# A graph layer and attention in float32: block products of the projections replaced by float32r products

## The chip, the cores and the metric

The kernel runs on one core of a Trainium2 chip. The metric is device time in microseconds from launch to end, as the median of several runs. The engines are TensorE (PE, with its weight loads shown as PEld), VectorE (DVE), ScalarE (ACT), GpSimd (POOL) and SyncE (SP), which issues most DMAs.

## What is computed

Input are 64 batches of 256 nodes with 512 features, and one graph of 256 nodes. Two layers follow, each with a residual and a layer norm. Cut to what matters:

```
# layer 0
mi, mj = x @ Wi.T, x @ Wj.T
out = deg * (mi + b) + adj @ mj
x = layernorm(x + out)
# layer 1, 8 heads of 64
q, k, v = (split_heads(x @ W.T + b) for W, b in ((Wq, bq), (Wk, bk), (Wv, bv)))
scores = where(adj == 0, -inf, q @ k.T / 8)
out = (softmax(scores) @ v) @ Wo.T + bo
x = layernorm(x + out)
```

Everything is float32. The products with Wq, Wk, Wv and Wo are the projections q, k, v and o.

## The kernel before

Two batches form a group, and there are 32 groups. All loops are unrolled; the order of the instructions on TensorE is written out by hand, since `matmul` (L290) keeps each in program order. `in_order` does the same for an instruction of another engine; other instructions, passed through `anywhere` or not wrapped at all, are placed by the framework's scheduler.

**Layer 0** (`l0_steps`). Each batch makes mi and mj by block products in Strassen's manner: seven products (steps 1 to 7) in place of eight, over sums `xS` of blocks of the transposed x (`sum_x`) and combined weights `w0`. Steps 1 and 3 share a PSUM bank x, steps 4 and 6 a bank y, steps 5 and 7 a bank z, and step 2 has a bank w. There are three slots for such banks (`bank`), two double banks for scores (`score_banks`) and one for attention values (`value_bank`). mj is split into two float32r parts, hi and lo (`split`), which `neighbours` multiplies with the graph, also float32r. `take` and `give` add and normalise the result, and `send_h` sends it through DRAM so that it comes back in columns, which `turn_h` transposes on DVE into `hT`.

**Projections** (`pair_steps`, `qkv_steps`, `qk_steps`, `v_steps`, `o_steps`). A group's two batches are the two block rows of a matrix of 512 rows; each projection has seven block products again, over sums `hS` (for q, k, v) or `oS` (for o). The right factors are blocks of a weight or differences of blocks; `make_factors` makes the differences once and keeps them in DRAM. `bring` loads factors of 256 KB from DRAM in the order of `queue`, eight ahead, and each is used by one step. The results are put together from the banks and from kept partial products (tag u) by DVE, ACT and POOL.

**Attention** (`scores`, `values`, `divide_two`, `multiply`). For each pair of heads, w from 0 to 7 in a group: scores on TensorE, mask on DVE (L809), exponential on ACT (L813), sum of two key halves on POOL (L816); then the values, the denominators `den`, a reciprocal on DVE (L886), eight small DMAs that spread it over the partitions, and a product on POOL (L848).

**The main loop** runs over the groups: the attention of group g is mixed with layer 0 of group g+1, and after it stand o of group g and q, k, v of group g+1, mixed with the end of layer 0 of the group's second batch b2. The first group has a prologue, the last an end of its own.

Of the kernel before, what the change touches and what calls it, by code (L numbers as in the profile page):

```python
# [224 lines left out]
def unshifted_path(ctx, tc, flag, x, adj, wiT, wjT, b0, wqT, bq, wkT, bk, wvT, bv, woT, bo, out):  # L225
# [27 lines left out]
    AHEAD = 8  # L253
# [6 lines left out]
    p4 = ctx.enter_context(tc.tile_pool(name="p4", bufs=4))  # L260
    p6 = ctx.enter_context(tc.tile_pool(name="p6", bufs=6))
    stream = ctx.enter_context(tc.tile_pool(name="stream", bufs=AHEAD + 1))
# [35 lines left out]
    def load_x(b):  # L298
        if b < B:
            xh[b] = p6.tile([P, NT, D], F32, tag="xh", name="xh")  # L300
            nc.sync.dma_start(out=xh[b], in_=x[b].rearrange("(t p) d -> p t d", p=P))

    b_bc = p4.tile([P, D], F32, tag="u", name="b_bc")
# [20 lines left out]
    xT, xS, hT, hS, qT, kT, vv, aoT, oS = ({} for _ in range(9))  # L324


    ident = const.tile([P, P], F32, name="ident")
# [15 lines left out]
    aT = p3.tile([P, NT, N], F32, tag="pk", name="aT")  # L343
    deg = small.tile([P, NT], F32, tag="deg", name="deg")
# [16 lines left out]
    def check_graph():  # L361


        exact = p1.tile([P, NT, N], F32, tag="oS", name="exact")
        in_order(nc.vector.tensor_tensor(exact, aT, graph.bitcast(F32), ALU.not_equal))
        in_order(nc.vector.tensor_reduce(inexact, exact.rearrange("p t n -> p (t n)"), AX.X, ALU.max))
        in_order(nc.vector.tensor_scalar(maskT, aT, 0.0, MASK, ALU.is_equal, ALU.mult))
# [9 lines left out]
    def load_bias(b, name):  # L377
        t = const.tile([P, NC], F32, tag=name, name=name)
        nc.sync.dma_start(out=t, in_=b)
        d = const.tile([P, 2], F32, tag=name + "d", name=name + "d")  # L380
        return t, d

    bq_sb, bqd = load_bias(bq, "bq")
    bk_sb, bkd = load_bias(bk, "bk")

    def bias_steps():
        for t, d in ((bq_sb, bqd), (bk_sb, bkd)):
            in_order(nc.vector.tensor_sub(d, t[:, 2:4], t[:, 0:2]))

    bv_t = small.tile([P, NC], F32, tag="bvt", name="bv_t")  # L390
# [5 lines left out]
    def blocks_of(w):  # L396
        return (w.rearrange("(h c p) (j o) -> p h c j o", h=2, p=P, j=2) if w is woT else
                w.rearrange("(p h c) (j o) -> p h c j o", h=2, p=P, j=2))

    sources = {}  # L400
    for name, w in (("wq", wqT), ("wk", wkT), ("wv", wvT), ("wo", woT)):
        src = blocks_of(w)
        sources[name] = {B11: src[:, 0, :, 0], B21: src[:, 1, :, 0], B22: src[:, 1, :, 1]}


    def load_raw(w, tag):
        raw = p1.tile([P, 2, 2, 2, H], F32, tag=tag, name="raw")
        nc.sync.dma_start(out=raw.rearrange("p h c j o -> p (h c) (j o)"),
                          in_=w.rearrange("(c p) o -> p c o" if w is woT else "(p c) o -> p c o", p=P))
        return raw  # L410

    def make_factors(w, name, raw):
        kept = dram.tile([4, P, 2, H], F32, tag=name, name=name)
        t1, t2, t3, t4 = (p4.tile([P, 2, H], F32, tag="u", name="t") for _ in range(4))
        b11, b12, b21, b22 = (raw[:, h, :, j, :] for h in range(2) for j in range(2))
        for n, (t, p, m) in enumerate(((t1, b12, b11), (t2, b22, t1), (t3, b22, b12), (t4, b21, t2))):
            in_order(nc.vector.tensor_sub(t, p, m))
            nc.sync.dma_start(out=kept[n], in_=t)
        sources[name].update({T1: kept[0], T2: kept[1], T3: kept[2], T4: kept[3]})

    spread = p3.tile([P, NC, P], F32, tag="pk", name="spread")
# [3 lines left out]

    def fold_value_bias(raw):

        pb = score_bank("pb")
        for c in range(NC):
            h, kc = divmod(c, 2)  # L430
            matmul(pb, spread[:, c], raw[:, h, kc].rearrange("p j o -> p (j o)"),
                   start=(c == 0), stop=(c == NC - 1))
        nc.vector.tensor_add(bo_bc, pb, bo_bc)
# [4 lines left out]
    def bring():  # L438
        if queue:
            name, n = queue.pop(0)  # L440
            f = stream.tile([P, 2, H], F32, tag="factor", name="factor")
            nc.sync.dma_start(out=f, in_=sources[name][n])
            coming.append(f)

    def next_factor():
        f = coming.pop(0)
        bring()
        return f


    def norm_stats(t, order=anywhere):
# [3 lines left out]
        nc.vector.bn_aggr(mv, st)  # L455
        ve = small.tile([P, 1], F32, tag="ve", name="ve")
        nc.vector.tensor_scalar(ve, mv[:, 1:2], EPS, None, ALU.add)
# [3 lines left out]
        nc.gpsimd.tensor_tensor(rstd, ve, mhalf, ALU.pow)  # L461
# [40 lines left out]
    def l0_steps(b, late=False):  # L502
        banks, k = {}, {}
        order = in_order if late else anywhere
# [19 lines left out]
        def split(t):  # L524
            nc.scalar.copy(k["hi"][:, t, :], k["mj"][:, t, :])
            nc.gpsimd.tensor_tensor(k["lo"][:, t, :], k["mj"][:, t, :], k["hi"][:, t, :].bitcast(F32),
                                    ALU.subtract)

        def step1():
            product("x", raw(0, 0), B11, True)  # L530
            nc.scalar.copy(keeper("u1"), banks["x"])

        def step2():
            product("w", raw(1, 1), T4, True)
            add_scaled(1, banks["w"])

        def step3():
            product("x", raw(0, 1), B21, False)
            add_scaled(0, banks["x"])

        def step4():
            product("y", xS[b]["S2"], T2, True)
            nc.vector.tensor_add(keeper("u2"), banks["y"], k["u1"])

        def step5():
            product("z", xS[b]["S1"], T1, True)
            k["mj"] = p1.tile([P, NT, D], F32, tag="mj", name="mj")
            nc.vector.tensor_copy(k["mj"][:, 1, :], banks["z"])

        def step6():  # L550
            product("y", xS[b]["S3"], T3, False)
            nc.vector.tensor_add(keeper("u3"), banks["y"], k["u1"])
            nc.gpsimd.tensor_tensor(k["mj"][:, 1, :], k["mj"][:, 1, :], k["u3"], ALU.add)

# [3 lines left out]
            if not late:  # L558
                add_scaled(1, k["u3"])

        def step7():
            product("z", xS[b]["S4"], B22, False)
            order(nc.vector.tensor_add(k["mj"][:, 0, :], banks["z"], k["u2"]))
# [11 lines left out]
        def take(t):  # L575
            r = xh[b][:, t, :]
            if late and t == 1:
                in_order(add_scaled(1, k["u3"]))
            in_order(nc.vector.tensor_add(r, k["pa"][:, t, :], r))
            stats[t] = norm_stats(r, in_order)  # L580

        def give(t):
# [3 lines left out]
        return [step1, step2, step3, step4, step5, step6, step7, neighbours, lambda: take(1), lambda: take(0),  # L586
                lambda: give(1), lambda: send_h(b, 1), lambda: give(0), lambda: send_h(b, 0)]

    def new_h(g):
        hT[g] = p1.tile([P, NC, NB * N], F32, tag="hT", name="hT")  # L590
        hS[g] = pair_blocks(hT[g], "hS")

    def sum_h(g):
        for step in left_steps(hS[g], in_order):
            step()
# [3 lines left out]
    def send_h(b, t):  # L599
        i = b % NB  # L600
        if t == 1:
            h_cols[b] = dram.tile([D // P, N, P], F32, tag=f"h{i}", name="h_cols")
        nc.sync.dma_start(out=h_cols[b][:, t * P:(t + 1) * P, :].rearrange("q p n -> p q n"),
                          in_=xh[b][:, t, :].rearrange("p (q n) -> p q n", n=P))
        if t == 0:
            hB[b] = p1.tile([P, N // R, P], F32, tag="hB", name="hB")
            nc.sync.dma_start(out=hB[b].rearrange("p a n -> p (a n)"),
                              in_=h_cols[b].rearrange("q (r a) n -> (q r) (a n)", r=R))

    def turn_h(b):  # L610
        g, i = divmod(b, NB)
        if i == 0:
            new_h(g)
        transposed(hT[g][:, :, i * N:(i + 1) * N], hB.pop(b))
        if i == NB - 1:
            sum_h(g)

    def h_transpose(b, t, borrow=False):
# [4 lines left out]
        pt = (score_banks("pt_h")[:, 0, :] if borrow else bank("pt_h")).rearrange("p (c n) -> p c n", c=NC)  # L623
        for c in range(NC):
            transpose(pt[:, c, :], xh[b][:, t, :].rearrange("p (n c) -> p c n", c=NC)[:, c, :], ident)
        nc.scalar.copy(hT[g][:, :, i * N + t * P:i * N + (t + 1) * P], pt)  # L626
        if t == 0 and i == NB - 1:
            sum_h(g)
# [6 lines left out]
    def pair_blocks(m, tag):  # L635

        s = p1.tile([P, 4, 2, N], F32, tag=tag, name=tag)
        return left_blocks(m[:, 0:2, 0:N], m[:, 2:4, 0:N], m[:, 0:2, N:2 * N], m[:, 2:4, N:2 * N], s)

    def block_product(bank, left, right, flip, first):  # L640


        for m in range(2):
            ms = slice(m * P, (m + 1) * P)
            for kc in range(2):
                lhsT, rhs = (right[:, kc, ms], left[:, kc, :]) if flip else (left[:, kc, ms], right[:, kc, :])
                matmul(bank[:, m, :], lhsT, rhs, start=(first and m == 0 and kc == 0),
                                 stop=(m == 1 and kc == 1), skip_group_check=True)

    def pair_steps(left, flip, use, early=False):  # L650


        banks, keepers = {}, {}

        def new_keeper(name):
            pool, tag = (p3, "lu") if early and name == "u1" else (p4, "u")
# [461 lines left out]
```

## Time and profile before

| What | Value |
|---|---|
| median of 3 runs | 3070.72 us (3069.8 to 3071.19) |
| profiled execution | 3068.79 us |
| its span, first to last instruction | 3066.9 us |
| mean granted TensorE clock | 0.999 |
| DMA | 447.54 MB, 146 GB/s over the span |
| one turn of the main loop, from 1460.92 us | 94.4 us |

"Busy" is the time in which an engine runs at least one instruction; matmuls overlap in the pipeline, so the distance from the start of one to the start of the next is what one costs. In a group of instructions, the number after the bar is the busy time, then the mean length of one in ns, then the idle time of the engine just before, with what ended it.

### The profile page before, as it was taken

How to read it: one execution, taken by the hardware profiler on the slowest of the kernel's cores; microseconds unless marked ns; L12 is line 12 of the kernel's file. 1: busy time of each engine (PE TensorE's matmuls, PEld its weight loads, DVE VectorE, ACT ScalarE, POOL GpSimd, SP SyncE). 2: the span in 40 equal slices, each digit the busy share in tenths (PEclk: the TensorE clock that was granted, in tenths of full speed). 3: DMA queues.
4: the chain of work that ended last, by engine and by line, in shares of the span. 5: the costliest groups of instructions: out<-in, count | busy, mean ns of one | idle time of the engine just before them, and what ended most of it. 6: DMA issues, size and time to landing. Idle time of an engine off the chain costs nothing. (4 is left out here: it accounts for less than half of the span.)

```text
span 3066.9 us, 46810 instructions
## 1 busy us (share of the span) xinstructions
PE 3036.6 (99%) x16646; PEld 2124.6 (69%) x16646; DVE 2178.3 (71%) x3298; ACT 974.1 (32%) x1861; POOL 1519.5 (50%) x1255
## 2 busy tenths in 40 slices
PE   7999999999999999999999999999999999999998
PEld 4667766677766777666776667776677766677665
DVE  6776677766777667777677777677766777767775
ACT  2323333323333333332233332333333333323332
POOL 2544545544545445464454554454544546445453
PEclk9999999999999999999999999999999999999999
DMA  7455544455444555345553445544455444555333
GB/s 255 123 151 159 169 121 136 132 161 166 144 125 127 159 170 155 116 133 154 161 168 119 126 145 160 167 134 134 127 158 170 151 121 128 159 161 166 120 111 96
DMA packets 410411, 447.54 MB, mean 146 GB/s; under 512 B 40896, under 2 KB 300224, under 8 KB 409792
## 3 DMA queue, kind: packets, MB, share of 16 engines
q1 hardware_dynamic: 410176, 444.50, 48.8%
q8 instruction: 136, 2.23, 0.3%
q14 instruction: 99, 0.81, 0.1%
HBM read 340.79 MB, written 70.25 MB: 134 GB/s over the span
## 5 line engine op out<-in xcount | busy, mean ns | idle before, releaser
L461 POOL TENSOR_TENSOR rstd<-ve,mhalf 128x1 f32<-128x1 f32 x256 | 140.5, 552 | 707.3 <-DVE below L459 707.3
L816 POOL TENSOR_TENSOR pk<-pe 128x512 f32<-128x512 f32 x256 | 323.1, 1278 | 322.2 <-ACT pe L813 322.2
L290 PE MATMUL po<-w,xS 128*128 128x512 f32 x1024 | 462.2, 599 | 0.7 <-DVE xS L478 0.7
L290 PE MATMUL st<-hS,factor 128*128 128x256 f32 x2048 | 453.2, 379 | 1.5 <-DVE u L689 1.2
L290 PEld LDWEIGHTS st<-hS,factor 128*128 128x128 f32 x2048 | 388.4, 190 | 56.3 <-DVE xh L744 1.7
L813 ACT ACTIVATE pe<-pe 128x1024 f32<-128x1024 f32 x256 | 270.8, 1058 | 364.4 <-DVE pe L809 364.4
L290 PE MATMUL po<-w,xT 128*128 128x512 f32 x768 | 352.1, 601 | 14.8 <-DVE xS L477 9.3
L290 PE MATMUL st<-hT,factor 128*128 128x256 f32 x1536 | 352.5, 379 | 0.7 <-ACT hT L626 0.7
L290 PEld LDWEIGHTS po<-w,xS 128*128 128x128 f32 x1024 | 189.6, 190 | 235.6 <-issue 206.3
L809 DVE TENSOR_TENSOR pe<-ps,maskT 128x1024 f32<-128x1024 f32 x256 | 298.0, 1195 | 35.4 <-PE ps L290 35.4
L290 PEld LDWEIGHTS st<-hT,factor 128*128 128x128 f32 x1536 | 291.9, 190 | 41.8 <-ACT hT L626 0.9
L886 DVE RECIPROCAL rden<-den 128x256 f32<-128x256 f32 x127 | 222.5, 1752 | 76.6 <-PE den L290 73.6
L290 PEld LDWEIGHTS po<-w,xT 128*128 128x128 f32 x768 | 144.2, 191 | 181.9 <-issue 162.8
L887 POOL TENSOR_TENSOR rtot<-rtot,rden 128x256 f32<-128x256 f32 x127 | 106.8, 841 | 320.1 <-DVE rden L886 320.1
L290 PE MATMUL ps<-qT,kT 64*128 64x256 f32 x2048 | 265.0, 393 | 0.0
L290 PE MATMUL pav<-pe,v_sb 128*32 128x256 f32 x4096 | 248.4, 382 | 1.9 <-ACT pe L813 1.9
L290 PEld LDWEIGHTS ps<-qT,kT 64*128 64x128 f32 x2048 | 184.5, 186 | 78.1 <-issue 38.6
L744 DVE TENSOR_TENSOR xh<-st,xh 128x512 f32<-128x512 f32 x186 | 144.5, 777 | 132.2 <-PE st L290 132.2
L290 PE MATMUL st<-factor,hS 128*128 128x256 f32 x1024 | 234.8, 382 | 0.0
L290 PEld LDWEIGHTS pav<-pe,v_sb 128*32 128x32 f32 x4096 | 119.8, 110 | 164.3 <-issue 95.4
L290 PE MATMUL st<-factor,oS 128*128 128x256 f32 x992 | 224.2, 379 | 0.0
L290 PEld LDWEIGHTS st<-factor,hS 128*128 128x128 f32 x1024 | 192.1, 190 | 35.2 <-issue 10.6
(115 smaller groups left out, 4648.2 us busy)
## 6 DMA issues: line engine op xcount, KB each, us to landing
xB<-in_x_dram SPq DMA_DIRECT2D x256, 128.0 KB, 3.9
xh<-in_x_dram SPq DMA_DIRECT2D x64, 512.0 KB, 4.2
factor<-wq SPq DMA_DIRECT2D x128, 256.0 KB, 4.2
factor<-wk SPq DMA_DIRECT2D x128, 256.0 KB, 2.8
factor<-wv SPq DMA_DIRECT2D x128, 256.0 KB, 2.6
spread<-rden SPq DMA_DIRECT2D x1016, 32.0 KB, 1.9
factor<-wo SPq DMA_DIRECT2D x124, 256.0 KB, 3.2
h_cols<-xh SPq DMA_DIRECT2D x124, 256.0 KB, 3.0
```

Of the source, the lines that this page charges most:

```text
L290: in_order(nc.tensor.matmul(*args, **kw))
L461: nc.gpsimd.tensor_tensor(rstd, ve, mhalf, ALU.pow)
L744: nc.vector.tensor_add(dst, src, dst)
L809: nc.vector.tensor_add(pe.rearrange("p j t q -> p j (t q)"), ps.rearrange("p j t q -> p j (t q)"), maskT.rearrange("p t q -> p (t q)").uns ...
L813: in_order(nc.scalar.activation(flat, flat, AF.Exp, scale=QSCALE, accum_out=etot[:, NB * g + i, pr:pr + 1]))
L816: nc.gpsimd.tensor_tensor(pk, pe[:, :, 0, :], pe[:, :, 1, :], ALU.add)
L886: nc.vector.reciprocal(rden, den)
L887: nc.gpsimd.tensor_tensor(rtot, rtot, rden, ALU.add)
```

## The change

**Projections in three float32r products.** Each operand A is split into a head, A x (1 - 2^-13) rounded to float32r; a low part, A - head; and a diff, head x (1 + 2^-12) - A. A weight tile f holds, likewise, its head, its low part times 2^12 (lift), and lift - head. Two sums are made: X = head·f_head + low·f_lift and Y = diff·f_diff, and the result is X x (1 + 2^-12) + Y. Each of the three products is one float32r matmul of 512 columns; the block products, the sums hS and oS, the kept partial products and `make_factors` go. A weight tile is [128, 3, 512], 768 KB, and a ring of six such tiles is loaded ahead. In the first group `make` builds each tile on ACT and DVE from the raw weight, and stores it in DRAM; later groups load it.

**Who splits.** The head is made on ACT, diff on DVE, low on DVE or POOL. h now comes back from DRAM as two halves (two loads), and each half is transposed, then split.

**Layer 0** runs its products in the order 1, 2, 3, 4, 6, 5, 7, so that mj's first half is made by one DVE add from bank z and u3 (before: a copy and a POOL add). One of the two lo parts of a batch goes from POOL to DVE.

**Order.** Nearly all vector operations, and the DMA issues of factors and of h, are pinned to program order. Four of the eight spread DMAs of a group's last division are issued by ACT. The first products of the following group's first batch are brought forward into the present group's end, and the last product of k stands after the first two scores. The value bias is folded in the first turn of the main loop, no longer in the prologue. Buffers change: p1, p3 and p5 take over from p4 and p6, rden and spread have one buffer, pk two.

The core of the diff:

```diff
-            nc.vector.tensor_copy(k["mj"][:, 1, :], banks["z"])
+            in_order(nc.vector.tensor_add(k["mj"][:, 1, :], banks["z"], k["u3"]))
...
+    def split_head(parts, src):
+        in_order(nc.scalar.activation(parts[0], src, AF.Identity, scale=DOWN))
+
+    def split_diff(parts, src):
+        in_order(nc.vector.scalar_tensor_tensor(parts[2], parts[0].bitcast(F32), UP, src, ALU.mult, ALU.subtract))
+
+    def split_low(parts, src, engine):
+        in_order(engine.tensor_tensor(parts[1], src, parts[0].bitcast(F32), ALU.subtract))
...
+    def make(f, name, j):
+        head, lift, diff = (f[:, i, :].rearrange("p (c o) -> p c o", c=NC) for i in range(3))
+        low = p3.tile([P, NC, P], F32, tag="lu", name="low")
+        for cs, raw in pieces(name, j):
+            in_order(nc.scalar.activation(head[:, cs], raw, AF.Identity, scale=DOWN))
+            in_order(nc.vector.tensor_sub(low[:, cs], raw, head[:, cs].bitcast(F32)))
+            in_order(nc.scalar.activation(lift[:, cs], low[:, cs], AF.Identity, scale=LIFT))
+        in_order(nc.vector.scalar_tensor_tensor(diff, low, LIFT, head.bitcast(F32), ALU.mult, ALU.subtract))
+        nc.sync.dma_start(out=kept[name][j], in_=f.bitcast(F32))
...
+    def pair(kind):
+        if kind == "S":
+            both = score_banks("pxy")
+            return both[:, 0, :], both[:, 1, :]
+        return bank("px"), value_bank("py") if kind == "A" else bank("py")
+
+    def rows_of_product(banks, parts, t, f, c):
+        X, Y = banks
+        head, low, diff = (d[:, c, t * P:(t + 1) * P] for d in parts)
+        first, end = c == 0, c == NC - 1
+        matmul(X, head, f[:, 0, :], start=first, stop=False, skip_group_check=True)
+        matmul(Y, diff, f[:, 2, :], start=first, stop=end, skip_group_check=True)
+        matmul(X, low, f[:, 1, :], start=False, stop=end, skip_group_check=True)
...
+    def v_step(g, i, t, kind, last):
...
+            in_order(nc.scalar.activation(dst, X, AF.Identity, scale=UP))
+            in_order(nc.vector.tensor_add(dst, Y, dst))
...
+    def o_steps(g, kinds, between):
...
+            in_order(nc.vector.scalar_tensor_tensor(r, X, UP, r, ALU.mult, ALU.add))
+            in_order(nc.vector.tensor_add(r, Y, r))
...
+        o = o_steps(g, "SMAS", [lambda: split_three(*turn_h(b2, 1), nc.vector),
+                                lambda: split_three(*turn_h(b2, 0), nc.vector)])
+        o[0]()
+        split_three(*turn_h(b1, 1), nc.gpsimd)
+        o[1]()
+        split_three(*turn_h(b1, 0), nc.gpsimd)
+        run([o[2], v[0]])
+        sum_x(b3)
+        v[1]()
+        turn_x(b3 + 1)
+        run([v[3], v[2], end[0], q_[0], end[1], k[0], end[2], q_[1], end[3], k[1], end[4]])
```

## The prediction

> **What bounds the kernel now.** I read the page's busy times first, then the costliest groups, then TensorE's timeline over one loop turn, then the windows of that turn. Busy times and the groups of the projections (busy us, mean ns of one, idle before):
>
> ```profile
> PE 3036.6 (99%) x16646; PEld 2124.6 (69%) x16646; DVE 2178.3 (71%) x3298; ACT 974.1 (32%) x1861; POOL 1519.5 (50%) x1255
> ...
> L290 PE MATMUL st<-hS,factor 128*128 128x256 f32 x2048 | 453.2, 379 | 1.5 <-DVE u L689 1.2
> ...
> L290 PE MATMUL st<-hT,factor 128*128 128x256 f32 x1536 | 352.5, 379 | 0.7 <-ACT hT L626 0.7
> ```
>
> TensorE is never short of work: the groups hardly idle. But "busy" counts overlapping pipelines, so what one matmul costs is read from start to start, in the timeline (start us, length, instruction):
>
> ```profile
> 1462.57 0.58 PE L290 MATMUL pa<-hi,graph 128*128 128x512 f32 x1
> 1462.99 0.39 PE L290 MATMUL pa<-lo,graph 128*128 128x512 f32 x1
> ...
> 1464.39 0.40 PE L290 MATMUL pa<-lo,graph 128*128 128x512 f32 x1
> 1464.62 1.89 PE L290 MATMUL st<-hT,factor 128*128 128x256 f32 x8
> 1466.35 1.89 PE L290 MATMUL st<-factor,aoT 128*128 128x256 f32 x8
> 1468.07 5.34 PE L290 MATMUL st<-hT,factor 128*128 128x256 f32 x24
> 1473.25 1.89 PE L290 MATMUL st<-factor,aoT 128*128 128x256 f32 x8
> ```
>
> One plain float32 matmul is two instructions (layer 0 has 4 products x 2 chunks x 64 batches = 512 on xS, and the page counts 1024), and 8 instructions take 1.73 us, so 0.216 us for one with 256 columns. The float32r matmuls of `neighbours` (hi and lo against graph, 512 columns) are one instruction each: 7 from 1462.99 to 1464.62, 0.234 us each. That is the price on which the change rests. The windows show the turn: projections with b2's neighbours, then attention, then both (busy us of PE, PEld, DVE, ACT, POOL; clock; DMA share; GB/s):
>
> ```profile
> 1460.92:1513.37 52.45, 52.45 (x253) 45.57 (x250) 36.24 (x64) 16.08 (x33) 23.11 (x20) 1.00 0.71 207
> 1513.37:1555.29 41.92, 41.92 (x273) 20.82 (x271) 31.09 (x39) 14.22 (x26) 24.37 (x21) 1.00 0.24 69
> 1460.92:1555.29 94.37, 94.37 (x524) 66.39 (x520) 67.33 (x103) 30.31 (x59) 47.48 (x40) 1.00 0.50 146
> ```
>
> A turn takes 94.4 us and TensorE fills it; DVE, next, is at 71%. So the time is the sum of TensorE's start-to-start intervals, and a cut there counts as long as no other engine opens a hole.
>
> [...]
>
> **The change part by part.** Times are against the profiled execution: 3068.8 us, of which 3066.9 is the span; the median of the runs is 1.9 above it.
>
> **Projection matmuls.** Before: 2048+1536+1024+992+768+744 = 7112 instructions x 0.216 = 1536.2 us. After: a group of two batches needs 48 each for q, k and v (4 outputs x 4 chunks x 3 products) and 48 for o. 32 groups x 144 + 31 x 48 = 6096 x 0.234 = 1426.5 us. **Gain 109.7 us**; per turn 48.4 less 44.9, 3.5 us. The spacing of 234 is from the same form (512 moving columns, fresh weights each time), so I keep it[...]. The LDWEIGHTS (188 ns) still fits under it.
>
> **DVE, per group.** Off: eight sums hS and oS, six u adds, three more (L696), L700, each 0.69; L720 4 x 0.48; L744 5 x 0.69 + 1.22: 19.0 us. On: Y adds of q, k, v 12 x 0.69; o 4 x 0.75 + 4 x 0.69; `split_diff` of h 4 x 0.8 (bounds: 0.69 as a plain add, 1.03 as the slowest L521 from SBUF) and of ao 1.4 + 2 x 0.8; lows 4 x 0.69: 23 us. Net +4, so 67.3 to about 71.5 of a 92 us turn, 78%. Hidden by TensorE on average.
>
> **ACT, per group.** Off: L715 12 x 0.47, L733 and L747 4 x 0.59: 8.0. On: 8 x 0.7, 4 x 0.58, heads 4 x 0.58, 1.0, 2 x 0.58, four DMA issues of some 0.6 (SP's eight take 4.95 us): 14.8. From 30 to 37 of 92: hidden. Queued behind the four issues are `give2` and a head; o's second half needs that head some 3 us later than I find it ready, so this is nothing unless that slack goes.
>
> **POOL, per group.** Off: L697 3 x 1.27, L553 2 x 1.5, L750 and L751 3.6, one lo a batch 2 x 1.38: 13.2. On: lows 4 x 1.28 + 2.4: 7.5. From 47 to 42: hidden.
>
> **Layer 0 in the order 4, 6, 5, 7.** A copy (L548) becomes an add of the same 0.69; L553 leaves the way to hi. ACT waited 240 us in all for it, but TensorE waited only 0.2 us for lo, so: nothing.
>
> **DMA.** Before, 28 factors of 256 KB a turn; after, 16 of 768 KB: 7.3 to 12.6 MB, in all some 160 MB more, 447 to 610 MB, about 203 GB/s over the span against the 351 to 424 GB/s of the busiest early windows. The ring of six is short at one place: the third and fourth wv tiles can start only when o's second half lets go of wo tiles, some 6 us before v needs them. A transfer of 1.9 us at 400 GB/s plus the 2 us that even a 32 KB spread needs to land makes 4 to 5. Hidden, with 1 to 2 us of slack; at 250 GB/s it would stall up to 2 us.
>
> **SP's queue.** `send_h` issues two loads in place of one (some 0.35 us each), pinned behind the writes whose landing they wait for; behind them stand the wv tiles, which wait for o's second half anyway. By the 3.0 and 3.5 us of h_cols and hB they land some 4 us before b2's first transpose: hidden. The last spread's split between SP and ACT saves 2.5 us of a chain with 3 us of slack: nothing. The first group's writes of made tiles (12.6 MB for 4.2) share the prologue's DMA; in the 7 us below. `fold_value_bias` (8 x 0.43) moves from the prologue into the first turn: nothing.
>
> **Pins.** They cost nothing by themselves; they forbid the scheduler to fill a wait, so what a pinned engine waits for holds all behind it. Bounds: +0.3 us a turn won (scores are no longer cut in two by `neighbours`; LDWEIGHTS waited 0.4 us there, 31 times), to the losses of the next step. I take 0.2 won.
>
> **The new hole: from o to v.** v's first step follows o's last product at once on TensorE and reads the parts of b1's first rows. On DVE, pinned: o0's adds (1.3), transpose (1.05, half of 2.12), a wait for ACT's head (0.7), diff (0.8), o1's adds (1.3), again 1.05 + 0.7 + 0.8. DVE comes to o0's adds some 5 us after o0 starts, as before them stand reciprocal, `add2`, two stats and four other operations (12 us by these durations, counted from w = 6). 5 + 1.3 + 2.55 + 1.3 + 2.55 = 12.7 against o's 48 x 0.234 = 11.2, so v is held 0.6 to 1.5 us: I take 1.0 (bounds 0, if DVE comes early, and 3). v2 then needs a score bank that o's last add frees after two more splits and adds: 0.4 more (bounds 0 and 1.5). Together 1.4, less 0.2: 1.2 x 31 = **+37 us**.
>
> **Prologue.** `make` sends each of 16 tiles through ACT, DVE, ACT in turn: 0.6 + 0.7 + 0.6 and the hand-overs, 2 us. Before v's first product can end, four must be made: about 8 us, while before, projections ran from raw blocks here. Less the making of factors that goes (16 x 0.7 to 1.6 on DVE): **+7 us** (0 to 15).
>
> Sum: 3068.8 - 109.7 + 37 + 7 = 3003.1; with 1.9 to the median, **3005 us**.
>
> **The rivals.**
> (B) The cover holds: DVE reaches o's adds early and no hole opens. For it: DVE at 78%, and the old turn had no hole at 71%. 3068.8 - 109.7 + 0 to 15 + 1.9 = 2961 to 2976; I give it 2945 to 2985.
> (C) The factor stream comes late at wv, or the prologue takes its upper bound: 1 to 2 us a turn above my case, 3036 to 3064. For it: transfers three times as long in a ring of six; against: the rate shown.
> (D) Slower: the pinned DVE chain from o to v becomes the bound. It decides from (109.7 - 7)/31 = 3.3 us of hole a turn. Place: v's first and last step. Price at the upper bounds: 3.0 + 1.5 = 4.5 us a turn, 3068.8 - 109.7 + 140 + 7 + 1.9 = 3108 us. For it: L480, a DVE sum that reads SBUF twice, takes from 410 to 1516 ns in the trace, so such operations can stretch, and the change adds nine of them a turn; against: most of them stand where TensorE has work.
>
> **How the numbers follow.** My case (2985 to 3035) has 0.45, B 0.25, C 0.12, D 0.12, and 0.06 is within 0.2% of 3070.7, about what a measurement of this kernel can tell from no change. The range from 2948 to 3060 takes in my case, nearly all of B and most of C: 0.8. Faster is 0.45 + 0.25 + 0.12 = 0.82.
>
> **What would show it.** The profile after should have float32r projections at 0.234 us from start to start; a turn of 92.1 us; DVE at 76 to 79%; idle TensorE at v's first product, released by ACT, DVE or POOL parts of b1, and at v's last, released by an add to xh. Spacing over 0.25 us, or a hole over 3 us a turn, would make the forecast wrong; idle time before X of the third wv tile, released by a DMA, would be C.

## The result: slower by 8.7%, and the profile after

| | before | after |
|---|---|---|
| median | 3070.95 us | 3340.39 us (3335.6 to 3343.68) |
| ratio | 1 | 1.0875, 95% interval 1.0856 to 1.0894 |
| span of the profiled execution | 3066.9 us | 3333.7 us |
| mean granted TensorE clock | 0.999 | 0.949 |
| one turn, from the neighbours' first product to the next turn's | 94.4 us | 102.2 us |

The loss of 267 us in the span is made of three pieces, read from the starts of b2's neighbours' products: 230 in the 30 turns of steady state, 23 up to the second group's, 14 after the last.

Busy times of after and the two groups of the projections that answer to those of before (after the bar: busy us, mean ns of one, idle us just before them with what ended most of it):

```profile
PE 3045.5 (91%) x15630; PEld 1963.8 (59%) x15630; DVE 2250.9 (68%) x3475; ACT 1145.8 (34%) x1991; POOL 1420.2 (43%) x1124
...
L290 PE MATMUL pxy<-factor,hA 128*128 128x512 f32 x256 | 134.4, 525 | 176.8 <-DMA factor<-wv 104.0
...
L290 PE MATMUL px<-hA,factor 128*128 128x512 f32 x640 | 184.3, 410 | 0.0
```

TensorE fell from 99% to 91%. The instructions are as many as forecast to be left; what is new is idle time, and most of it stands at v: the first group, the head products of v, has 176.8 us, the second, a group of q and k, none. The windows of one turn (columns as before):

```profile
1596.63:1655.51 58.88, 51.37 (x201) 38.03 (x197) 36.44 (x65) 16.82 (x29) 22.96 (x17) 0.91 0.55 203
1655.51:1698.91 43.40, 43.14 (x294) 23.10 (x293) 32.98 (x42) 18.40 (x32) 21.70 (x18) 1.00 0.48 162
1596.63:1698.91 102.28, 94.50 (x493) 61.13 (x489) 69.42 (x107) 35.23 (x61) 44.66 (x35) 0.95 0.52 186
```

Seen against the three windows of before: attention is 1.5 us longer and the stage with the projections 6.4 us. Pieces of work changed sides between the two (k's last product and a pair of scores went to attention, two products of layer 0 left it), so only the sum, 7.9 us, is the change's. The idle time lies in the stage with the projections: 7.5 us, with the clock down to 0.91. TensorE's timeline in this stage, at the change from o to v:

```profile
1609.54 0.39 PE L290 MATMUL py<-factor,kT 128*128 128x512 f32 x1
1609.76 0.39 PE L290 MATMUL px<-factor,v 128*128 128x512 f32 x1
...
1613.16 0.39 PE L290 MATMUL pxy<-factor,v 128*128 128x512 f32 x1
1615.78 0.50 PE L290 MATMUL pxy<-factor,hA 128*128 128x512 f32 x1 [2.23 <-ACT hA L593]
...
1617.63 0.50 PE L290 MATMUL pxy<-factor,hL 128*128 128x512 f32 x1 [0.62 <-POOL hL L599]
...
1622.76 0.80 PE L290 MATMUL pxy<-factor,hA 128*128 128x512 f32 x1 [3.48 <-DMA factor<-wv]
1623.36 0.63 PE L290 MATMUL pxy<-factor,hD 128*128 128x512 f32 x1
1623.78 0.63 PE L290 MATMUL pxy<-factor,hL 128*128 128x512 f32 x1
```

In o (the first two lines) one float32r product follows the other after 0.227 us. Then come two holes: 2.2 us ahead of v's first product, which waits for the head of h, and 3.5 us ahead of its third factor, which waits for the wv tile. After them a product takes 0.43 us (1623.36 to 1623.78), at half clock (0.50 from 1622 to 1624). Why the tile is late is in SyncE's queue, the DMA issues in the same microseconds:

```profile
1605.31 4.37 SPq L616 DMA_DIRECT2D h_cols<-xh  x2
1615.09 0.81 SPq L620 DMA_DIRECT2D hB<-h_cols  x2
1615.99 0.86 SPq L428 DMA_DIRECT2D factor<-wv  x2
1616.94 0.38 SPq L428 DMA_DIRECT2D factor<-wq  x1
1617.41 0.38 SPq L428 DMA_DIRECT2D factor<-wk  x1
```

and what released the hB load at 1615.09 is the end of this VectorE instruction, b1's last transpose, at 1613.95 + 1.11 = 1615.06:

```profile
1613.95 1.11 DVE L483 STREAM_TRANSPOSE hF<-hB 128x512 f32<-128x512 f32 x1
```

hB has one buffer (pool p1). The load of b2's half may not overwrite it before b1 has been transposed out of it. SP waits there, and the wv tiles behind it, pinned, start at 1615.99 and land at 1622.7 and 1624.6, though o's second half had let go of the first wo tile at about 1610 (in run 5 below the same two tiles are issued from 1610.07 on).

### The profile page after: what moved, and what is told of

Read it like the earlier page. It is cut to its first block, busy times and chain, and to the rows that moved or that the text cites. A ratio compares the mean times of both kernels' runs of the same rounds, so it can differ in the third digit from the quotient of the medians.

```text
span 3333.7 us, 43827 instructions
## 1 busy us (share of the span) xinstructions
PE 3045.5 (91%) x15630; PEld 1963.8 (59%) x15630; DVE 2250.9 (68%) x3475; ACT 1145.8 (34%) x1991; POOL 1420.2 (43%) x1124
## 5 line engine op out<-in xcount | busy, mean ns | idle before, releaser
L290 PE MATMUL po<-w,xS 128*128 128x512 f32 x1024 | 481.6, 603 | 2.4 <-DVE mj L550 2.0
L290 PE MATMUL pxy<-factor,hA 128*128 128x512 f32 x256 | 134.4, 525 | 176.8 <-DMA factor<-wv 104.0
L684 DVE TENSOR_TENSOR kT<-py,kT 128x512 f32<-128x512 f32 x128 | 88.5, 691 | 276.1 <-ACT kT L683 276.1
L804 POOL TENSOR_TENSOR aoT<-aoT,spread 128x512 f32<-128x512 f32 x127 | 167.1, 1316 | 175.5 <-DMA spread<-rden 159.3
L465 ACT ACTIVATE xh<-xh,shift,rstd 128x512 f32<-128x512 f32 x256 | 208.7, 815 | 8.5
L593 ACT ACTIVATE hA<-hF 128x512 fp32r<-128x512 f32 x124 | 78.1, 630 | 379.6 <-DVE hF L483 379.6
L290 PEld LDWEIGHTS pxy<-factor,hA 128*128 128x128 f32 x256 | 57.3, 224 | 239.6 <-DMA factor<-wv 147.3
L290 PE MATMUL px<-hA,factor 128*128 128x512 f32 x640 | 184.3, 410 | 0.0
L290 PE MATMUL py<-hD,factor 128*128 128x512 f32 x640 | 175.4, 396 | 5.1 <-ACT kT L683 5.1
L599 POOL TENSOR_TENSOR v<-aoT,qT 128x512 fp32r<-128x512 f32 (+1 forms) x93 | 169.1, 1818 | 23.0 <-ACT qT L593 23.0
```

What stands on the lines that cost most here:

```text
L290: in_order(nc.tensor.matmul(*args, **kw))
L465: order(nc.scalar.activation(t, t, AF.Identity, bias=shift, scale=rstd))
L593: in_order(nc.scalar.activation(parts[0], src, AF.Identity, scale=DOWN))
L599: in_order(engine.tensor_tensor(parts[1], src, parts[0].bitcast(F32), ALU.subtract))
L684: in_order(nc.vector.tensor_add(dst, Y, dst))
L804: in_order(nc.gpsimd.tensor_tensor(d, d, spread, ALU.mult))
```

## The experiments

The theory from this trace: **the pinned order on SP**. A pinned load stands behind an issue that waits for a single buffer. Its rivals: the added **volume** (610 MB for 447) makes the tiles late; the **VectorE chain** from o to v sets the time (rival D of the forecast); the **half clock** is a loss of its own. Turn lengths below are medians over the trace, read like those above. "Ratio" is the time over that of the kernel before, measured beside it, with its 95% interval in brackets; the indented text is what was expected before the run.

**1. The loads last** (e1_load_behind), b2's two hB loads behind all four factor loads of o's second half:

```diff
-        if t == 0:
...
+        if t == 0 and i == 0:
+            fetch_h(b)
...
                 bring()
+            fetch_h(NB * (g + 1) + 1)
```

`fetch_h` holds the two hB loads; the second call is that for b2.

> The two loads of b2's h are issued behind o's factor loads instead of ahead of them; nothing else changes. Queue theory (b2's loads wait on SP for the only hB buffer, and the wv tiles stand behind them): the wv tiles start some 4 to 6 us earlier, the hole inside v's first step (3.5 us and more) goes and with it most of the half clock; the turn falls from 102.4 to about 97 us, the time to 3150 to 3200 us. Bandwidth theory (tiles of 768 KB land late however early they are issued): within 50 us of 3340. Vector theory (the chain of DVE operations from o to v is the hole): within 50 us of 3340.

Measured 3442.33 us, ratio 1.1213 [1.1194, 1.1232], turn 105.8 us. A miss on the wrong side. The wait for wv is gone from the list of waits; in its place VectorE waits 164 us in all for hB, and TensorE is idle for 4.0 us a turn ahead of the products of q (0.7 in after).

**2. The turns first** (e2_turn_first), b1's two transposes and splits ahead of o's adds on VectorE, all else as in the changed kernel:

```diff
-        o[0]()
         split_three(*turn_h(b1, 1), nc.gpsimd)
-        o[1]()
         split_three(*turn_h(b1, 0), nc.gpsimd)
+        o[0]()
+        o[1]()
```

> b1's two transposes and splits stand ahead of o's first two additions on DVE instead of between them; the issue order of DMAs is untouched. Vector theory: v starts without its wait of about 3 us and the turn loses all of its hole, 3050 us or less. Queue theory: hB comes free some 6 us earlier, so the wv tiles start about 2 us earlier, and 3 us at v's start go, but a hole of 2 to 3 us inside v's first step stays: 3180 to 3260 us. Bandwidth theory: 3 us a turn at most, 3240 us or more.

Measured 3273.63 us, ratio 1.0665 [1.0642, 1.0689], turn 100.6. Faster than after, but above the queue theory's range and inside that of the bandwidth theory: the hole at wv stays (3.20 and 0.92 us in one turn). The start of v is idle for 1.7 us; the profile names no releaser, but the last add of o[0], which now stands behind the turns and frees the score bank, ends 0.1 us before it.

**3. Both** (e3_both).

> Both of the former. Queue and vector theory together: the holes of v's first step go, no half clock is left, and the turn is 91 to 93 us: 2960 to 3020 us, faster than the kernel before. Bandwidth theory: the wv tiles still land after they are needed, 3150 us or more.

Measured 3433.99 us, ratio 1.1195 [1.1164, 1.1225]: a clear miss, so the theory as it stood was too narrow. The holes of one turn in TensorE's timeline:

```profile
1670.09 0.77 PE L290 MATMUL px<-factor,hA 128*128 128x512 f32 x1 [4.68 <-DVE xh L711]
...
1688.12 1.64 PE L290 MATMUL pxy<-hA,factor 128*128 128x512 f32 x4 [4.49 <-DVE ve L455]
```

The first is b2's v: the add that is named stands on VectorE behind b2's transpose, which waits for hB, and hB, issued behind four tiles of 768 KB, lands 7.7 us after its issue (median for b2). The second, ahead of q[1], I overlooked at this point. The number alone would fit the bandwidth theory, but no product waits for a wv tile in the turns of this run.

**4. Nothing pinned on SP** (e4_dma_unpinned):

```diff
-                in_order(nc.sync.dma_start(out=f.bitcast(F32), in_=kept[name][j]))
+                nc.sync.dma_start(out=f.bitcast(F32), in_=kept[name][j])
```

and the same for the h_cols writes and the hB loads.

> The issues of the factor loads and of h's stores and loads are left to the scheduler, as in the kernel before; all other pins stay. The scheduler then puts two wv loads ahead of b2's h loads. Queue theory: like the kernel with the loads behind, 3150 to 3220 us, and the pin of the DMA issues is what costs. If the pin doesn't matter: within 50 us of 3340.

Measured 3173.6 us, ratio 1.0335 [1.0318, 1.0353], turn 96.6: a hit. The scheduler's order was wv, wv, hB, hB, wq, wk. No wait for wv is left, with the same bytes. In SP's queue:

```profile
1630.34 1.44 SPq L428 DMA_DIRECT2D factor<-wv  x2
1635.68 0.80 SPq L620 DMA_DIRECT2D hB<-h_cols  x2
...
1648.38 0.32 SPq L428 DMA_DIRECT2D factor<-wq  x1
1649.07 0.32 SPq L428 DMA_DIRECT2D factor<-wk  x1
1652.06 2.55 SPq L310 DMA_DIRECT2D xB<-in_x_dram  x4
```

**5. That order, pinned** (e5_order_pinned): as in 1, but `fetch_h` is called after the second `bring()` of o's last step.

> Of the changed kernel only the place of b2's two hB loads in SP's pinned order is altered: they come after the second wv tile and before wq and wk (in the changed kernel before all four, in the run that put them last after all four). Bytes, tiles and all other orders stay. Theory of the queue (the wv tiles are late because their issue stands behind a load that waits for the single hB buffer; h itself is late if 1.5 MB of wq and wk stand ahead of it): like the run with the DMA issues unpinned, 3150 to 3200 us, no wait for wv of over 1 us a turn. Rival, pinning as such costs (the scheduler's freedom was what the unpinned run gained by): 3250 to 3340. Rival, volume (610 MB can't be carried beside the products): no change, 3320 to 3350.

Measured 3335.84 us, ratio 1.0863 [1.0845, 1.0881], turn 102.3: no gain at all, so the first theory was not enough; the number alone would fit either rival. TensorE's timeline shows v without a wait for wv, and a new hole, ahead of q[1]:

```profile
1634.64 1.07 PE L290 MATMUL px<-hL,factor 128*128 128x512 f32 x4
1639.68 2.05 PE L290 MATMUL pxy<-hA,factor 128*128 128x512 f32 x4 [3.97 <-DVE st L451]
```

The releaser named there, a VectorE statistic, had long been done. The other operand is the second wq tile, and SP's queue says when it was issued:

```profile
1615.40 0.80 SPq L623 DMA_DIRECT2D hB<-h_cols  x2
1616.29 0.38 SPq L428 DMA_DIRECT2D factor<-wq  x1
1616.76 0.38 SPq L428 DMA_DIRECT2D factor<-wk  x1
1631.74 2.55 SPq L310 DMA_DIRECT2D xB<-in_x_dram  x4
1634.39 0.55 SPq L428 DMA_DIRECT2D factor<-wq  x1
```

It stands behind xB's four loads. xB, too, has one buffer, and its loads wait for VectorE's transpose of the batch before, which in program order (`turn_x(b3 + 1)`) comes ahead of v[2], whose four `bring()` load these tiles. In the changed kernel this delay is hidden: v ends 5.3 us later there, and q[1] waits 0.55 us. So the gain at wv was given back at the next place of the same kind. The misses above (1, 3, 5) have this in common; run 4 had escaped it because the scheduler put two of these loads ahead of xB's, as its lines show.

**6. The turns early** (e6_turn_early): from 5, give2(0) and its write ahead of a head on ScalarE, both transposes of b1 ahead of o's adds, first the half that v[0] reads.

```diff
         multiply()
-        split_head(*ao_parts(g, 1, lower))
         give2(0)
         send_h(b2, 0)
+        split_head(*ao_parts(g, 1, lower))
...
+        h0, h1 = turn_h(b1, 0), turn_h(b1, 1)
+        split_head(*h0)
+        split_head(*h1)
+        split_diff(*h0)
...
         o[0]()
-        split_three(*turn_h(b1, 1), nc.gpsimd)
         o[1]()
-        split_three(*turn_h(b1, 0), nc.gpsimd)
```

> The order of loads of the run before this one, and besides: give2(0) and its write ahead of the lower head's copy on ScalarE, both transposes of b1 ahead of o's adds on VectorE, the half of b1 that v[0] reads first. Theory (what is left is v[0]'s start, which waits for hA of a half whose transpose stands behind o[0]'s and o[1]'s adds, some 2.5 us a turn with the slow clock after it): 3030 to 3110 us. Rival (the start of v[0] then waits for the score bank that o[0]'s adds let go of, or o[2] for its lower parts): 3140 to 3200, and the wait shows under that name.

Measured 3348.62 us, ratio 1.0906 [1.0887, 1.0924]: a miss. The hole ahead of v[0] shrank to 0.2 us, but the time was given back ahead of q[1] (a hole of 4.3 us in one turn) and at v's later products, which wait 2.5 us a turn for banks that o's second pair of adds frees. xB's loads, in the way still, took back what was gained ahead of them.

**7. Zeros in the hole** (e7_zeros_in_hole): the changed kernel with 14 products of a zero tile ahead of v[0]'s third factor. They add nothing to the sum.

```diff
+                if g and (i, t, c) == (0, 0, 2):
+                    for _ in range(14):
+                        matmul(X, zero, coming[1][:, 0, :], start=False, stop=False, skip_group_check=True)
```

> The changed kernel with 14 more float32r products of a zero tile into v[0]'s bank ahead of its third factor, in the hole where it waits for wv; they add nothing to the sum. 14 x 0.23 = 3.2 us of TensorE work a turn in a hole of about 4. Theory of the clock (TensorE's clock is halved for some 10 us because of the hole, and the slots after it cost 0.43 in place of 0.23): the half clock after 1622 in the turn goes, 13 slots x 0.2 = 2.6 us a turn, 3250 to 3290 us with a granted clock of 0.97 or more. Rival (the half clock comes from elsewhere, the transfers or the first hole of v[0]): no gain, the zeros run at 0.43 and last 6 us: 3350 to 3420.

Measured 3304.61 us, ratio 1.0775 [1.0737, 1.0814], clock 0.973: 36 us less than after, where the theory said 50 to 90. The zeros themselves run mostly at half clock (14 in 5.13 us, at a clock of 0.57 from 1604 to 1608), and the clock is back at full before the real products go on (1.00 from 1608, the first of them at 1608.60). The windows of the changed kernel and then of this one, four or two microseconds each (the clock is the third number from the end):

```profile
1616.00:1618.00 2.00, 1.15 (x4) 0.51 (x4) 0.53 (x2) 0.00 (x0) 1.58 (x1) 1.00 0.79 281
1618.00:1620.00 2.00, 1.28 (x4) 0.49 (x2) 1.30 (x2) 0.63 (x1) 0.00 (x0) 0.54 0.99 381
...
1626.00:1628.00 2.00, 2.00 (x6) 1.51 (x6) 1.67 (x3) 0.60 (x1) 0.00 (x0) 0.50 0.13 52
```

```profile
1604.00:1608.00 4.00, 4.00 (x12) 3.10 (x11) 3.48 (x5) 0.45 (x1) 0.00 (x0) 0.57 0.97 324
1608.00:1612.00 4.00, 4.00 (x19) 3.09 (x18) 3.61 (x6) 0.78 (x2) 0.00 (x0) 1.00 0.80 330
```

So part of the loss is the clock: the hole was paid a second time in the products after it. That the transfers cause it is refuted, since in the later window they go on at 330 GB/s and the clock is full.

**8. v[0] and v[1] side by side** (e8_pair): from 6, factors 0 and 1 for both, then 2 and 3.

> The kernel with early turns and the loads in the new order, and besides v[0] and v[1] side by side: factors 0 and 1 for both, then factors 2 and 3 for both, so that two products of some 1.4 us each stand before the first use of the third wv tile in place of one. Theory: what wait for wv is left (0 to 1.5 us a turn) goes: 10 to 50 us under the run with early turns. Rival: no wait for wv is left there, and v[1]'s parts, needed 1.4 us sooner, are late: same or up to 30 us slower.

Measured 3352.19 us, ratio 1.092 [1.0902, 1.0939]. Inside the rival's range, but inconclusive: like 6, it ends ahead of q[1] (4.96 us).

**9. xB's loads behind v[2]'s** (e9_xb_behind), from 5:

```diff
-        turn_x(b3 + 1)
-        run([v[3], v[2], end[0], q_[0], end[1], k[0], end[2], q_[1], end[3], k[1], end[4]])
+        run([v[3], v[2]])
+        turn_x(b3 + 1)
+        run([end[0], q_[0], end[1], k[0], end[2], q_[1], end[3], k[1], end[4]])
```

> The pinned loads in the order wv, wv, hB, wq, wk, as in the run that came out no faster than the changed kernel, and one more step moved: turn_x(b3 + 1), whose xB loads wait for the single xB buffer and so for VectorE's transpose, comes after v[2] and so behind v[2]'s four factor loads on SP. Theory of the queue in its second form (a pinned load stands behind any issue that waits for a single buffer: with the wv hole closed, the next such place, wq behind xB, gave the 4.0 us hole ahead of q[1] and the half clock after it): the hole goes, 6.5 us a turn, 3120 to 3180 us, near the unpinned run. Rival (610 MB are at the limit there, and a load that comes earlier only makes another late): 3280 to 3340.

Measured 3161.79 us, ratio 1.0298 [1.028, 1.0315], turn 96.5: a hit, 174 us under 5 by one step moved. With all loads pinned and all bytes carried, both rivals of run 5 fall: neither pinning as such nor the volume made that loss. The step moves xB's transpose (2.1 us) on VectorE too, and no run parts the two, but the tile that q[1] waited for in run 5 was issued behind xB's loads. The theory holds in its second form, for two places where a pinned load stood behind an issue that waits for a single buffer; the first hid the second (the second alone was not opened in any run). What is left is the hole from o to v (us in all, times, longest):

```profile
PE pxy L290 <- ACT hA L593: 70.5, 32, 3.0
PE pxy L290 <- POOL hL L599: 17.2, 31, 0.6
```

**10. The adds first** (e10_adds_first): 6 with 9's step, and o's second pair of adds ahead of b2's turns on VectorE.

```diff
             for t in range(NT):
-                between[t]()
                 add(1, t, banks[t])
+            for t in range(NT):
+                between[t]()
```

> The kernel with early turns, xB's loads behind v[2]'s as in the run before this one, and o's second pair of adds ahead of b2's two turns on VectorE (they waited there for hB to land, while v[1] and v[2] waited for the banks). Theory: from the run before this one, v[0]'s start (3.1 us and 2 us of half clock a turn) goes and 1.2 us of wait for wv come: 3000 to 3060 us. Rival (h of b2, whose loads land behind 1.5 MB of wv, makes v[3] wait): 3080 to 3150, with a wait of VectorE for hB and of TensorE for hA at v[3].

Measured 3078.23 us, ratio 1.0029 [1.0016, 1.0041], turn 93.6, clock 0.995. A near miss by 18 us, 2 us short of the rival's range; the waits that the rival names do not show (VectorE waits 0.6 us in all for hB). The holes at v shrank to 1 us and less, and the half clock went with them: it is 1.00 in all 30 turns. What is left of them has a cause I had not counted. VectorE, and beside it GpSimd, in the same microseconds:

```profile
1576.56 1.37 DVE L596 SCALAR_TENSOR_TENSOR hD<-hA,hF 128x512 fp32r<-128x512 f32 x1 [0.16 <-ACT hA L593]
1577.86 1.77 DVE L596 SCALAR_TENSOR_TENSOR kT<-qT,aoT 128x512 fp32r<-128x512 f32 x1
1579.56 1.77 DVE L596 SCALAR_TENSOR_TENSOR hD<-hA,hF 128x512 fp32r<-128x512 f32 x1
```

```profile
1576.09 1.30 POOL L599 TENSOR_TENSOR v<-aoT,qT 128x512 fp32r<-128x512 f32 x1 [0.75 <-ACT qT L593]
1577.33 3.45 POOL L599 TENSOR_TENSOR hL<-hF,hA 128x512 fp32r<-128x512 f32 x2
```

The same difference takes 0.69 us where GpSimd is idle (in after, at 1619.74). In these lines GpSimd's operation began first. In after, at 1608.28, VectorE's began first and kept to 0.69 us, and GpSimd's subtraction, begun at 1608.32, took 1.80 in place of 1.29.

**11. The pair on top** (e11_pair_first).

> As the run before this one, with v[0] and v[1] side by side. Theory: the 1.2 us wait for wv goes as well: 10 to 50 us under it, 2970 to 3040 us. Rival: v[1]'s banks, let go by the adds only at some 4 us after o's end, take its place: the same within 10 us.

Measured 3077.47 us, ratio 1.0024 [1.0014, 1.0035]: the rival's "same within 10 us". The wait for wv went, v[3]'s parts came late instead.

**12. Without GpSimd's low parts of b1** (e12_no_pool_share), from 11:

```diff
-        split_diff(*h0)
         split_diff(*ao_parts(g, 1, lower))
         split_low(*ao_parts(g, 1, lower), nc.gpsimd)
-        split_low(*h0, nc.gpsimd)
-        split_diff(*h1)
-        split_low(*h1, nc.gpsimd)
+        split_diff(*h0)
+        split_low(*h0, nc.vector)
...
         o[0]()
+        split_diff(*h1)
+        split_low(*h1, nc.vector)
         o[1]()
```

> The pair kernel with one more reordering: the lower difference goes first of the three on VectorE, and the two low parts of b1 move from GpSimd to VectorE (0.69 us each there), the second half's parts behind o[0]'s adds. In the run before, VectorE's differences beside GpSimd's low parts took 1.36 to 1.77 us in place of 0.69, and v[0]'s start, o[2]'s lower products and v[3] waited 1.26, 0.65 and 1.0 us a turn. Theory (VectorE's operation waits until GpSimd's is done, and that makes the chain from o to v late): 1.5 to 2.5 us a turn less, 3000 to 3030 us, below the kernel before. Rival (the same work on VectorE is as late, since its queue is longer by 1.4 us a turn): 3065 to 3085 us, no change, with the holes where they were.

Measured 3072.56 us, ratio 1.0009 [1.0002, 1.0015]. The number is the rival's, though 5 us under 11: the hole at o[2]'s lower products went, and new ones came at v[1] (0.4 us a turn). Of the three differences two still take 1.67 and 1.22 us beside GpSimd operations, the third 0.68, and VectorE has more to do.

**13. More bytes** (e13_more_bytes), on top of 9:

```diff
                 in_order(nc.sync.dma_start(out=f.bitcast(F32), in_=kept[name][j]))
+                again.append(again.pop(0))
+                in_order(nc.sync.dma_start(out=again[0], in_=kept[name][j][:, 0]))
```

> The kernel with both loads moved (wv, wv, hB, wq, wk and xB behind v[2]'s four), 3162 us, with 256 KB more to carry behind each of the 496 pinned factor loads: a copy of the tile's first third to a place in device memory that nothing reads, 130 MB in all, about what the change added to the transfers (163 MB). Theory of the queue (where the issues stand made the loss, the bytes fit beside the products): the tiles land 0.6 us later each, most of it hidden; up to 1.5 us a turn, 3155 to 3210 us. Rival (the volume is what makes the factors late, and the reordering only shifted it): 2 us or more for each group of four tiles, waits for wv, wq and wk throughout the projections, 3300 us or more.

Measured 3250.47 us, ratio 1.0595 [1.0579, 1.0611], turn 99.4. Between the two expectations, so neither is right: 129 MB more read, and as much written, cost 89 us, 3 us a turn. The waits that grew are not for wv: TensorE waits 14.0 us in all for wq (13 times), and waits for smaller loads, queued among the large tiles, grow (us in all, times, longest):

```profile
POOL aoT L809 <- DMA spread<-rden: 168.5, 83, 4.4
DVE hF L483 <- DMA hB<-h_cols: 53.8, 31, 2.3
```

in run 9, and here, where the code stands three lines lower:

```profile
POOL aoT L812 <- DMA spread<-rden: 321.5, 89, 8.1
DVE hF L486 <- DMA hB<-h_cols: 84.2, 31, 3.9
```

The weight loads of layer 0's products also wait longer for mj (54 us in all for 18). The 496 extra issues on SP, 0.5 us each, are part of this cost; the run does not tell them from the bytes.

**14. The shorter chain** (e14_short_chain), from 12: the last low part of ao on VectorE, the sum into rtot behind v's pair.

> From the version that came out level with the kernel before (3073 us): the last low part of ao moves from GpSimd to VectorE and the rtot sum behind v's pair, so that nothing of GpSimd's stands beside VectorE's three differences (1.67 and 1.22 us there, 0.69 alone). VectorE's chain from the differences to v[3]'s parts, 0.65 us shorter. Theory (that chain is what now bounds the stretch from o to v): 0.5 to 1.2 us a turn less, 3035 to 3058 us, under the kernel before. Rival (something else sets it, such as hB's landing for b2 or the wv tiles): 3068 to 3078 us.

Measured 3065.83 us, ratio 0.9993 [0.9985, 1.0001], turn 93.3. A miss by 8 us, between the two ranges. The difference takes 0.65 us now, but the next wait shows at once, one that the rival names:

```profile
1581.68 0.50 PE L290 MATMUL pxy<-factor,hA 128*128 128x512 f32 x1 [1.14 <-DMA factor<-wv]
```

The gain was 0.2 us a turn; then wv, which can be loaded only when o lets go of a tile in the ring of six, is last. This is the best version, and within 0.2% of the kernel before: it does not beat it.

TensorE's idle time in one turn, by the product that it stands ahead of, and the granted clock, both as means over the 30 steady turns of each trace, sum up the way (us; the rest of the turn has at most 0.1):

| run | at o | at v | at q and k | clock |
|---|---|---|---|---|
| after | 0.6 | 6.4 | 0.7 | 0.95 |
| 5, hB's loads moved | 0.6 | 3.0 | 3.6 | 0.95 |
| 9, xB's moved too | 0.7 | 3.1 | 0.0 | 0.98 |
| 10, VectorE reordered too | 1.5 | 0.8 | 0.0 | 1.00 |
| 14 | 0.5 | 1.4 | 0.0 | 1.00 |

## Why the prediction was wrong, step by step

**The failed step is "SP's queue".** It said of the factor tiles that "behind them stand the wv tiles, which wait for o's second half anyway", and "hidden". It priced the landing of hB and overlooked that hB has one buffer for b1 and b2, so that its second load waits for a VectorE instruction; the wv tiles stood behind that wait from about 1610 to 1615.99. The same holds for xB at wq, a step the forecast never looked at. Both together are worth 179 us: after 3340, run 9, which changes no work and moves two places in SP's order (with xB's transpose on VectorE), 3162. Opening hB's alone gave nothing (run 5). The forecast's own paragraph on pins says that what a pinned engine waits for holds all behind it; it was not applied to SP.

**"The new hole: from o to v"** had the mechanism right and the size wrong. It took 1.0 us at v's start, with 3 as the upper bound; the trace after has 2.23 + 0.22 + 0.62 = 3.1. Reordering VectorE, ScalarE and GpSimd (run 10 against 9) gave 2.9 us a turn, 84 us, the half clock after the hole included. This cause alone is enough for a loss: run 9, which has it and no longer SP's, is 92 us slower than the kernel before. Rival D was thus right in place and sign for this half of the loss; its price, 3108 us, is 54 below run 9 and has no half clock in it, and it did not see SP's half. Rival B, no hole at all, fell. Runs 9 and 10 together give back 262 of the 269 us between the medians, by order alone.

**The half clock** is missing from the forecast altogether. In the turn shown of after the clock is 0.50 from 1618.17 to 1628.41, for 10.24 us, and of the 38 stretches at half clock in that trace 27 are as long, the others 3.41 to 13.65 us. Ahead of the one shown TensorE was idle in three pieces, 2.23, 0.22 and 0.62 us with two products of 0.50 us between them; the hole of 3.48 us lies inside it. In the turn shown of run 7, with zeros in that hole, the half clock lasts some 6.9 us (0.57 in each of the two windows of 4 us from 1600 to 1608). Run 9, where v still waits for its head (70.5 us in all) and its low part (17.2), has a mean of 0.973 over its span; run 10, where those waits shrank, has 0.995, and a turn of run 14 (1560 to 1653) 1.00. Run 7 recovered 36 us of this; how much of the loss is clock in all was not measured apart.

**Projection matmuls**: 6096 instructions, right; 0.234 us was too much for a long row, the trace has 0.227 (the prediction's own lines give 0.233), so the gain by spacing is 1536 - 1384 = 152 us and not 110, 4.9 us a turn. Of these 4.9 us run 14, at full clock, keeps 1.2 (the mean of its turns against that of before). 2.0 are idle time, and the other 1.7 or so fit the longer distances around its waits: 0.3 to 0.7 us from one start to the next, where the records count 0.2 us of idle time or none.

**"DMA"**: 610 MB, right. "4 to 5" us for the landing of a wv tile was right for a first tile with no load just ahead of it (4.7 in run 5), and short behind hB's two loads: issued at 1615.99, the first landed at 1622.7, the second 1.9 us later. "Hidden" failed by the issue first, and by the landing in runs 10 and 14. The sign that the prediction gives for rival C, idle time before the third wv tile, stands in the trace after, but at 3.4 us a turn and by SP's order, where C has 1 to 2 by the tiles' landing; C describes what is left in run 14, some 1 us. More volume is not free, as run 13 shows, but runs 9 and 10 carry all 610 MB. (The upper end of its range is 3067 by its own sum, not 3064; nothing hangs on it.)

**DVE, ACT, POOL by busy time**: 69.4, 35.2 and 44.7 us a turn for 71.5, 37 and 42, near enough. The average was the wrong question: VectorE is at 68% and yet late in the 16 us from the neighbours' sum (1600.0) to v's start (1615.8).

**Layer 0's order, nothing**: no new wait stands at its products in the steady turns (idle time before the xS products is 2.4 us in the whole run). **Pins, 0.2 us won**: wrong in sign on SP, where the order that they fixed cost 167 us (run 4 against after); pinned in a better order, run 9, the kernel is 12 us faster than with the scheduler's (run 4).

**Prologue**: +7 was forecast (0 to 15), +23 measured up to the second group, the first turn included. The end, which the forecast left out, is 14 us longer in after and 7 in run 14. Neither was taken apart by a run; what of it is `make`'s chain stays open. With 23 and 7 lost there, run 14 wins 36 us in its turns, and that is why it is only level. Its 61 us above the forecast are its turns (93.2 for 92.1, 34 us), 16 of the prologue and 7 of the end.

## What to carry to other kernels

Before pinning a DMA queue, write down for every issue in it which buffer it overwrites and who reads that last: here a load into a single buffer held all that stood behind it, whatever their own buffers allowed. When a stall's removal brings nothing, look for the next one of the same kind before dropping the theory; here the second place showed only once the first was open. And count the slack of the stretch in which a gain falls anew before booking it: here a faster o and v moved the deadline of VectorE and of the wv tiles, which feed them.

## What the runs showed of the hardware that was not expected

- A float32r product of 512 columns takes 0.227 us in a long row, less than the 0.233 to 0.234 of the neighbours' products.
- VectorE's difference (L596, 128x512) takes 0.65 to 0.69 us alone, and up to 1.77 beside a GpSimd operation that began first; in the lines of run 10 it then ends 0.5 to 0.6 us after GpSimd's instruction does (1577.93 after 1577.39, 1581.33 after 1580.78). Where VectorE's began first it kept to 0.69 and GpSimd's took 1.80 in place of 1.29 (after). In run 12 the difference took 1.67 us beside a GpSimd operation, in run 14, with nothing of GpSimd's beside it, 0.65.
- Tiles of 768 KB queued one behind the other land 1.9 us apart (1622.7 and 1624.6 in after), and a load of 256 KB behind four of them lands 7.7 us after its issue (median for b2 in run 3; 5.4 for b1 and b2 together) where the median in after is 2.9.
